# One more gate set in the recurrence of a four-layer kernel, one layer matrix made eleven batches earlier, and one batch's outputs issued in two pairs

## The chip, the core and the metric

The kernel runs on one core of a Trainium2 chip. A core has five engines with instruction streams of their own: TensorE (PE in the profile, with its weight loads shown apart as PEld), VectorE (DVE), ScalarE (ACT), GpSimd (POOL) and SyncE (SP), which here only issues DMA transfers. Each engine takes its instructions in the order in which they were written for it, and they wait for each other through semaphores. All matrices are in 32-bit floats, and the profile shows each such matrix product twice: four products of the program are eight PE instructions in a row.

The metric is the time of one execution on the device in microseconds (us), as the median of several runs.

## The reference

The input x has 16 batches of 512 steps with 512 features each; a condition vector of 512 numbers belongs to each batch. Four layers follow each other, each with a residual: x = x + layer(x, cond).

- L0 scales x by a gate that is worked out from the condition. (Its wavelet transform and the inverse, with one gate for all levels, come to v * gate; the layer has a residual of its own, so x is multiplied by 2 + gate.)
- L1 is a recurrence over the 512 steps: h = tanh(x_t Wx + h Wh + b), with the condition as the first h.
- L2 has three products per batch: f = sigmoid(x Wf + bf), i = sigmoid(x Wi + bi), c = x Wc + bc. With s = f + i, it takes f/s and i/s, multiplies i/s by c, and runs a product over time backwards and a sum over time forwards to get a hidden state per step.
- L3 makes one 512 x 512 matrix per batch, base + A B, where A and B (rank 8) come from a small network on the condition, and multiplies x by it.

## The kernel before

**Phase 1, the recurrence (lines 543 to 677).** The order on PE, ACT, DVE and SP is the order of the program, written out by hand. The 512 steps are 64 blocks (index n) of 8 steps (s). In every step PE issues 16 products h Wh (`accumulate`, L417), ACT takes the tanh (L609) and DVE transposes the result into the next h (L610); then PE may go on with the next step. Between two steps PE is given other work:

- `inputs` (L426 to L432, recorded at L417 too): x Wx for the next block. `SHARE` says how many of its 16 groups go into each step; from block 17 on they are the odd steps 1, 3, 5 and 7, 16 products each.
- `early_gate` (L445 to L522): gate products of L2, for steps of the sequence that are done already. `SETS` lists them: each set is (batches, steps, chunk of 128 features), and has 12 slots, four for f, four for i, four for c. A slot is four products of 32 columns of weights by 512 columns (L465). `PARTS` says in which steps of a block a slot is issued. Before, they are steps 0, 2, 4 and 6 in blocks 17 to 62, and 0, 2, 3, 4 and 6 in block 63.

The elementwise work of a set is cut into pieces for DVE (L488 to L512: two sums, eight inversions of 64 columns, four normalizations, two products with the candidate), and `do_pieces` issues one per step, or two in blocks 62 and 63. The sigmoids on ACT are timed: that of f six steps after its last slot, that of i in the step of its last slot. What is done is written to a DRAM tile `early` with rows of TE steps (L483, on SP's queue). When the last step is over, the pieces that are left are issued, and then `add_base` (L537) for the first batch's L3 matrix.

**Phase 2, batch by batch (lines 680 to 812).** Here a planner orders each engine's instructions. For each of the 16 batches b and each chunk j of 128 features, `gate_unit(b, j, x3)` issues 12 products on PE over the steps that phase 1 did not do (L700; `te` is the number of steps done early), loads the early ones (L715, SP), takes two sigmoids (L716, ACT), and then ten instructions on DVE from L717 to L732, among them a reciprocal (L718) and three scans; two additions on POOL (L736, L737) give `x3`.

Between the units:

- `layer_rows(b)` loads the factors of batch b's L3 matrix (L527, L528, SP) into `at` and `bt`, which have one buffer each.
- `layer_of(b)` (L744) makes the matrix after unit 2: four products into the PSUM banks pl0, pl1, po0 and po1 (L535), and four additions of the base on DVE (`add_base`, L539), which free the banks again.
- `last_layer` (L760) multiplies the previous batch's x3 by its matrix: four tiles of 128 steps, four products each (L756), in turns into the banks po0 and po1; ACT copies each out (L751), SP stores it (L752).

`last_layer` of batch b - 1 stands after unit (b, 1). Batch 15 differs: its own matrix is made after unit (15, 0), in place in `base_sb`, and the outputs of batch 14 stand after unit (15, 3). The outputs of batch 15 follow, three of the four chunks first, the last chunk when DVE has it.

Of the kernel before, what the change touches and what calls it, by code (L numbers as in the profile page):

```python
# [35 lines left out]
P = 128  # L36
B, S, D = 16, 512, 512
KC = D // P
R = 8

T = 8
NBLK = S // T
# [14 lines left out]
FIRST, SECOND, MAIN = 16 // T, 32 // T, 128 // T + 1  # L57
# [3 lines left out]
SETS += [(slice(b, b + 4), slice(0, 128), j) for b in (0, 4) for j in range(KC - 2)]  # L61
SETS += [(slice(b, b + 4), slice(16, 144), KC - 2) for b in (0, 4, 8, 12)]
SETS += [(slice(b, b + 4), slice(32, 160), KC - 1) for b in (0, 4, 8, 12)]
SETS += [(slice(b, b + 4), slice(64, 192), j) for b in (8, 12) for j in (0, 1)]

PARTS = [()] * FIRST + [(0, 1, 3, 4, 5, 7)] * (SECOND - FIRST) + [(0, 2, 4)] * (MAIN - SECOND) + [(0, 2, 4, 6)] * (NBLK - MAIN - 1) + [(0, 2, 3, 4, 6)]
TE = 192


def made_before(b, j):  # L70
# [13 lines left out]
def kernel(  # L84
# [360 lines left out]
    def early_gate(q, step):  # L445
# [32 lines left out]
        def sigmoid(gate, bias):  # L478
            nc.scalar.activation(gate, ps, AF.Sigmoid, bias=col(bias, j))
# [33 lines left out]

        if which == 0:

            timed.setdefault(step if first else step + 6, []).append(lambda: sigmoid(f, C_BF))
        elif which == 1:
            timed.setdefault(step, []).append(end_input_gate)
        else:

            assert not any(job in pieces for job in early_gate.sums)
            urgent.extend(lambda at=at: times_candidate(at) for at in halves)  # L522
# [168 lines left out]
    def bank(tag, name):  # L691
        return pools[tag].tile([P, D], F32, tag=tag, name=f"{tag}_{name}")
# [56 lines left out]
    def leave(b, t, po, tag="osb"):  # L749
        osb = work.tile([P, D], F32, tag=tag, name=f"osb_{b}_{t}")  # L750
        nc.scalar.copy(osb, po)  # L751
        nc.sync.dma_start(out=out[b, t * P : (t + 1) * P, :], in_=osb)  # L752

    def output_part(po, t, x3, layer, ks):
        for k in ks:
            nc.tensor.matmul(  # L756
                po, x3[:, k, t * P : (t + 1) * P], layer[:, k, :], start=(k == 0), stop=(k == KC - 1)
            )

    def last_layer(b, x3, layer):  # L760
        for t in range(S // P):
            po = bank(f"po{t % 2}", f"{b}_{t}")
            output_part(po, t, x3, layer, range(KC))
            leave(b, t, po)

    layer = wx_sb
    pending = None
    for b in range(B):
        x3 = x3pool.tile([P, KC, S], F32, tag="x3", name=f"x3_{b}")
        end = b == B - 1  # L770
        if 0 < b < B - 1:
            factors = layer_rows(b)
        for j in range(KC):
            gate_unit(b, j, x3)
            if j == (KC - 1 if end else 1) and pending is not None:
                last_layer(*pending)
            if j == 2 and 0 < b < B - 1:
                layer_of(b, *factors, layer)
            if j == 0 and end:

                layer_of(B - 1, *layer_rows(B - 1), base_sb)
        pending = b, x3, layer


# [5 lines left out]
    def last_rows(ks, n):  # L790
        for k in ks:
            nc.tensor.matmul(
                ends[n],
                x3[:, k, last * P :],
                base_sb[:, k, columns[n]],
                start=(k == 0),
                stop=(k == KC - 1),
            )

    for t, po in enumerate(pos):  # L800
        output_part(po, t, x3, base_sb, range(KC - 1))
    for n in range(2):
        last_rows(range(KC - 1), n)

    for t, po in enumerate(pos):
        output_part(po, t, x3, base_sb, (KC - 1,))
        leave(B - 1, t, po, ("osb", "i", "s")[t])
    for n, copy in enumerate((nc.vector.tensor_copy, nc.scalar.copy)):
        last_rows((KC - 1,), n)
# [61 lines left out]
```

## Time and profile before

The kernel before took 1618.64 us (median of 3 runs, 1617.01 to 1619.62). The profiled execution took 1615.84 us; its span, from the first to the last instruction, is 1614.1 us.

| what | us |
|---|---|
| phase 1, to the first product of unit (0, 0) at 909.40 | 909.4 |
| phase 2, from there to the end of the span | 704.7 |
| PE busy | 1603.6 (99%) |
| DVE busy | 1132.3 (70%) |
| ACT busy | 424.9 (26%) |
| POOL busy | 172.6 (11%) |

In a line of the profile's timeline stand the start in us from the span's start, the length in us, the engine, the source line, the operation, what it writes <- what it reads (partitions x elements) and how many such instructions are merged (x); brackets at the end name the idle time before and what ended it. L417 is line 417 of the kernel before. The end of a product is modelled, so the distance from one start to the next is what is read from PE's rows, not the length. "PEclk" is the clock that was granted to TensorE, 1.00 being full.

### The profile page before, as it was taken

How to read it: one execution, taken by the hardware profiler on the slowest of the kernel's cores; microseconds unless marked ns; L12 is line 12 of the kernel's file. 1: busy time of each engine (PE TensorE's matmuls, PEld its weight loads, DVE VectorE, ACT ScalarE, POOL GpSimd, SP SyncE). 2: the span in 40 equal slices, each digit the busy share in tenths (PEclk: the TensorE clock that was granted, in tenths of full speed). 3: DMA queues.
4: the chain of work that ended last, by engine and by line, in shares of the span. 5: the costliest groups of instructions: out<-in, count | busy, mean ns of one | idle time of the engine just before them, and what ended most of it. 6: DMA issues, size and time to landing. Idle time of an engine off the chain costs nothing.

```text
span 1614.1 us, 67901 instructions
## 1 busy us (share of the span) xinstructions
PE 1603.6 (99%) x29328; PEld 1146.0 (71%) x29328; DVE 1132.3 (70%) x3618; ACT 424.9 (26%) x2484; POOL 172.6 (11%) x145
## 2 busy tenths in 40 slices
PE   9999999999999999999999999999999999999998
PEld 6888888888888888888888655555555555555564
DVE  4555655565556666666665798888888888988887
ACT  3333333333333333333333211111111111111111
POOL 0000000000000000000000022222222222222222
PEclk9999999999999999999999999999999999999999
DMA  7554431111111111111111101111111111111111
GB/s 228 148 147 128 121 105 46 36 31 36 37 37 37 37 37 37 37 37 31 37 39 30 29 21 43 33 43 39 43 40 44 44 46 39 31 44 47 37 44 58
DMA packets 128085, 88.11 MB, mean 55 GB/s; under 512 B 22645, under 2 KB 116633, under 8 KB 127785
## 3 DMA queue, kind: packets, MB, share of 16 engines
q1 hardware_dynamic: 79152, 55.05, 11.1%
q10 hardware_dynamic: 48632, 28.73, 6.2%
q8 instruction: 229, 3.75, 1.0%
q14 instruction: 72, 0.58, 0.1%
HBM read 55.67 MB, written 28.07 MB: 52 GB/s over the span
## 4 chain that ended last, share of the span: by engine, by line
PE 96%; DVE 2%; DMA 1%; issue 0%; SPq 0%; ACT 0%; ACTq 0%; DVEq 0%
PE pre L417 41%; PE po L756 13%; PE pg L465 13%; PE pf L700 9%; PE pc L700 9%; PE pi L700 9%; PE pf L380 1%; PE pl_layer L535 1%; DVE s L718 1%; DMA wh_sb<-in_wh_dram 1%; PE pl_last L756 0%; DMA xb<-in_xT_dram 0%; DVE s L726 0%; DVE s L730 0%; PE po_last L756 0%
## 5 line engine op out<-in xcount | busy, mean ns | idle before, releaser
L417 PEld LDWEIGHTS pre<-wh_sb,h_out 128*32 128x32 f32 x16384 | 466.7, 110 | 146.6 <-DVE h_out L610 143.4
L417 PE MATMUL pre<-wh_sb,h_out 128*32 128x128 f32 x16384 | 560.6, 273 | 2.4 <-DVE h_out L610 1.1
L610 DVE STREAM_TRANSPOSE h_out<-a 128x32 f32<-128x32 f32 x2048 | 264.6, 187 | 347.4 <-ACT a L609 345.9
L609 ACT ACTIVATE a<-pre 128x32 f32<-128x32 f32 x2048 | 238.0, 203 | 573.4 <-PE pre L417 572.7
L417 PE MATMUL pre<-wx_sb,x 128*32 128x128 f32 x8192 | 285.9, 273 | 1.0 <-DMA wx_sb<-in_wx_dram 0.5
L417 PEld LDWEIGHTS pre<-wx_sb,x 128*32 128x32 f32 x8192 | 239.0, 110 | 2.1 <-DMA wx_sb<-in_wx_dram 1.5
L756 PE MATMUL po<-wx_sb,x 128*128 128x512 f32 x480 | 209.0, 592 | 0.1
L756 PEld LDWEIGHTS po<-wx_sb,x 128*128 128x128 f32 x480 | 91.0, 190 | 111.6 <-issue 105.7
L700 PE MATMUL pf<-x,wf_sb 128*128 128x352 f32 (+3 forms) x512 | 165.3, 466 | 0.3 <-DVE x L622 0.3
L700 PE MATMUL pc<-x,wc_sb 128*128 128x352 f32 (+3 forms) x512 | 163.7, 463 | 1.3 <-DVE i L722 1.3
L700 PE MATMUL pi<-x,wi_sb 128*128 128x352 f32 (+3 forms) x512 | 163.6, 462 | 0.0
L718 DVE RECIPROCAL s<-s 128x368 f32<-128x368 f32 (+2 forms) x64 | 152.2, 2378 | 2.2
L700 PEld LDWEIGHTS pf<-x,wf_sb 128*128 128x128 f32 x512 | 96.0, 190 | 68.4 <-issue 15.8
L736 POOL TENSOR_TENSOR s<-s,f 128x512 f32<-128x512 f32 x63 | 86.5, 1374 | 509.9 <-DVE s L730 504.1
L700 PEld LDWEIGHTS pc<-x,wc_sb 128*128 128x128 f32 x512 | 97.2, 190 | 57.5 <-DVE i L722 1.9
L700 PEld LDWEIGHTS pi<-x,wi_sb 128*128 128x128 f32 x512 | 97.3, 190 | 55.9
L622 DVE TENSOR_TENSOR x<-x,h_out 128x128 f32<-128x128 f32 x256 | 101.2, 395 | 18.9 <-DMA wi_sb<-in_wiT_dram 0.2
L751 ACT COPY osb<-po 128x512 f32<-128x512 f32 x60 | 35.1, 585 | 263.4 <-PE po L756 144.9
L683 POOL MEMSET zero<- 128x1 f32 x1 | 0.1, 98 | 907.5 <-DVE wx_sb L539 907.5
L717 DVE SCALAR_TENSOR_TENSOR s<-f,i 128x368 f32<-128x368 f32 (+2 forms) x64 | 34.7, 543 | 88.1 <-ACT i L716 88.1
L716 ACT ACTIVATE f<-pf,vec_sb 128x368 f32<-128x368 f32 (+2 forms) x64 | 35.7, 558 | 215.2 <-PE pf L700 160.6
L465 PE MATMUL pg<-x,wc_sb 128*32 128x512 f32 (+1 forms) x640 | 84.2, 581 | 0.0
(113 smaller groups left out, 1270.8 us busy)
## 6 DMA issues: line engine op xcount, KB each, us to landing
out_dram<-osb SPq DMA_DIRECT2D x63, 256.0 KB
xb<-in_xT_dram ACTq DMA_DIRECT2D x61, 256.0 KB
w<-in_l3w_dram SPq DMA_DIRECT2D x72, 128.0 KB
w<-in_l3w_dram ACTq DMA_DIRECT2D x64, 128.0 KB
early<-ef SPq DMA_DIRECT2D x39, 128.0 KB
early<-ei SPq DMA_DIRECT2D x39, 128.0 KB
f<-early SPq DMA_DIRECT2D x16, 96.0 KB
i<-early SPq DMA_DIRECT2D x16, 96.0 KB
```

The lines of the kernel that those rows point to most:

```text
L417: nc.tensor.matmul(pre[PLACE[g][0]][j * BP : (j + 1) * BP, PLACE[g][1], :], lhsT, tile_columns(w, j), start=False, stop=False, skip_group_ ...
L465: nc.tensor.matmul(ps[c * BP : (c + 1) * BP, :].rearrange("p (b t) -> p b t", **shape), w[:, k, j * P + c * BP : j * P + (c + 1) * BP], x2 ...
L609: nc.scalar.activation(a[:, at], pre[bank][:, place, at], AF.Tanh)
L610: nc.vector.transpose(turned[:, c, :], a[:, at])
L622: nc.vector.tensor_tensor(x2[:, :, :, at].rearrange("p k b t -> p k t b"), xs[n][:, :, t0 // 2, :, :], turned.rearrange("p k (t b) -> p k ...
L700: nc.tensor.matmul(p[:, te:], w_sb[:, k, j * P : (j + 1) * P], x2[:, k, b, te:], start=(k == 0), stop=(k == KC - 1),)
L716: nc.scalar.activation(gate[:, new], p[:, new], AF.Sigmoid, bias=col(bias, j))
L717: nc.vector.scalar_tensor_tensor(s[:, new], f[:, new], EPS, i[:, new], ALU.add, ALU.add)
L718: nc.vector.reciprocal(s[:, new], s[:, new])
L736: engine.tensor_tensor(s, s, f, ALU.add)
L751: nc.scalar.copy(osb, po)
L756: nc.tensor.matmul(po, x3[:, k, t * P : (t + 1) * P], layer[:, k, :], start=(k == 0), stop=(k == KC - 1))
```

## The change

1. **One more set**, (batches 4 to 7, steps 128 to 255, chunk 0), the seventeenth of now 21. Its 12 slots go into step 7 of blocks 53 to 62, beside the input products that are there, and into steps 1 and 5 of block 63. `made_before(b, 0)` is 256 rather than 128 for these four batches. TE grows from 192 to 256. As the slots of a set now follow each other more closely, the sigmoid of f comes at the latest one step before the first slot of the set's third gate.
2. **The matrix of batch 15** is made in batch 4, after unit (4, 0), and put into `x2[:, :, 0, :]`, the place of batch 0's input to L2; `layer_rows(15)` stands at the head of batch 4. `layer_rows(b)` of the batches 1 to 14 now comes after unit (b, 0).
3. **The outputs of batch 14** stand in two pairs of tiles, after the units (15, 1) and (15, 2). In every batch the products of the first two tiles are interleaved: three of tile 0, two of tile 1, the last of tile 0, the last two of tile 1.

```diff
+SETS += [(slice(4, 8), slice(128, 256), 0)]
 SETS += [(slice(b, b + 4), slice(64, 192), j) for b in (8, 12) for j in (0, 1)]
-PARTS = ... + [(0, 2, 4)] * (MAIN - SECOND) + [(0, 2, 4, 6)] * (NBLK - MAIN - 1) + [(0, 2, 3, 4, 6)]
-TE = 192
+PARTS = ... + [(0, 2, 4)] * (MAIN - SECOND)
+PARTS += [(0, 2, 4, 6)] * (NBLK - MAIN - 11) + [(0, 2, 4, 6, 7)] * 10 + [tuple(range(T - 1))]
+TE = 256
+SLOTS = [n * T + s for n in range(NBLK) for s in PARTS[n]]
+FIRST_PARTS = SLOTS[::KC]
...
-            timed.setdefault(step if first else step + 6, []).append(lambda: sigmoid(f, C_BF))
+            late = step if first else min(step + 6, FIRST_PARTS[u + 2] - 1)
+            timed.setdefault(late, []).append(lambda: sigmoid(f, C_BF))
...
-    def last_layer(b, x3, layer):
-        for t in range(S // P):
-            po = bank(f"po{t % 2}", f"{b}_{t}")
-            output_part(po, t, x3, layer, range(KC))
-            leave(b, t, po)
+    def last_layer(b, x3, layer, rows):
+        t = rows[0]
+        po = [bank(f"po{n}", f"{b}_{t + n}") for n in range(2)]
+        ahead = 0 if t else 2
+        output_part(po[0], t, x3, layer, range(KC - 1))
+        output_part(po[1], t + 1, x3, layer, range(ahead))
+        output_part(po[0], t, x3, layer, (KC - 1,))
+        leave(b, t, po[0])
+        output_part(po[1], t + 1, x3, layer, range(ahead, KC))
+        leave(b, t + 1, po[1])
...
+    last_matrix = x2[:, :, 0, :]
+    when = ({1: ((0, 1), (2, 3))}, {1: ((0, 1),), 2: ((2, 3),)})
...
-        if 0 < b < B - 1:
-            factors = layer_rows(b)
+        extra = layer_rows(B - 1) if b == KC else None
         for j in range(KC):
             gate_unit(b, j, x3)
-            if j == (KC - 1 if end else 1) and pending is not None:
-                last_layer(*pending)
+            if extra and j == 0:
+                layer_of(B - 1, *extra, last_matrix)
+            if j == 0 and 0 < b < B - 1:
+                factors = layer_rows(b)
+            if pending is not None:
+                for rows in when[end].get(j, ()):
+                    last_layer(*pending, rows)
             if j == 2 and 0 < b < B - 1:
                 layer_of(b, *factors, layer)
-            if j == 0 and end:
-                layer_of(B - 1, *layer_rows(B - 1), base_sb)
```

In the last outputs `last_matrix` stands for `base_sb`.

More of the change, by code (lines that the diff above doesn't have):

```diff
@@ L63 @@
 SETS += [(slice(b, b + 4), slice(32, 160), KC - 1) for b in (0, 4, 8, 12)]
+SETS += [(slice(4, 8), slice(128, 256), 0)]
 SETS += [(slice(b, b + 4), slice(64, 192), j) for b in (8, 12) for j in (0, 1)]
-PARTS = [()] * FIRST + [(0, 1, 3, 4, 5, 7)] * (SECOND - FIRST) + [(0, 2, 4)] * (MAIN - SECOND) + [(0, 2, 4, 6)] * (NBLK - MAIN - 1) + [(0, 2, 3, 4, 6)]
-TE = 192
+PARTS = [()] * FIRST + [(0, 1, 3, 4, 5, 7)] * (SECOND - FIRST) + [(0, 2, 4)] * (MAIN - SECOND)
+PARTS += [(0, 2, 4, 6)] * (NBLK - MAIN - 11) + [(0, 2, 4, 6, 7)] * 10 + [tuple(range(T - 1))]
+TE = 256
+SLOTS = [n * T + s for n in range(NBLK) for s in PARTS[n]]
+FIRST_PARTS = SLOTS[::KC]
+assert len(SLOTS) == 3 * KC * len(SETS)
 def made_before(b, j):
@@ L794, in last_rows @@
                 x3[:, k, last * P :],
-                base_sb[:, k, columns[n]],
+                last_matrix[:, k, columns[n]],
                 start=(k == 0),
@@ L800 @@
     for t, po in enumerate(pos):
-        output_part(po, t, x3, base_sb, range(KC - 1))
+        output_part(po, t, x3, last_matrix, range(KC - 1))
     for n in range(2):
@@ L805 @@
     for t, po in enumerate(pos):
-        output_part(po, t, x3, base_sb, (KC - 1,))
+        output_part(po, t, x3, last_matrix, (KC - 1,))
         leave(B - 1, t, po, ("osb", "i", "s")[t])
```

## The prediction

> **What bounds the kernel now.** I read the page's busy shares first, then the chain, then the timeline of PE with that of DVE beside it.
>
> ```profile
> PE 1603.6 (99%) x29328; PEld 1146.0 (71%) x29328; DVE 1132.3 (70%) x3618; ACT 424.9 (26%) x2484; POOL 172.6 (11%) x145
> PE 96%; DVE 2%; DMA 1%; issue 0%; SPq 0%; ACT 0%; ACTq 0%; DVEq 0%
> ```
>
> PE is never without work, and 96% of the chain is PE: what the change adds to PE, or makes PE wait for, goes into the time in full. Next, three steps of the recurrence, and one without a filler near its end:
>
> ```profile
> 863.73 1.09 PE L417 MATMUL pre<-wh_sb,h_out 128*32 128x128 f32 x32
> 864.61 1.07 PE L465 MATMUL pg<-x,wc_sb 128*32 128x512 f32 x8
> 865.47 1.09 PE L417 MATMUL pre<-wh_sb,h_out 128*32 128x128 f32 x32
> 866.34 1.09 PE L417 MATMUL pre<-wx_sb,x 128*32 128x128 f32 x32
> 867.21 1.09 PE L417 MATMUL pre<-wh_sb,h_out 128*32 128x128 f32 x32
> ...
> 896.77 1.09 PE L417 MATMUL pre<-wh_sb,h_out 128*32 128x128 f32 x32
> 898.40 1.08 PE L417 MATMUL pre<-wh_sb,h_out 128*32 128x128 f32 x32 [0.54 <-DVE h_out L610]
> ```
>
> A gate slot takes 0.86 us (864.61 to 865.47), input products 0.87; a step with either is 1.74 us long, a bare one 1.63. So the way over ACT and DVE hides 0.75 us of filler, and one filler already uses it up.
>
> In phase 2 the timelines of PE and DVE belong together (batch 4 starts at 1074.48):
>
> ```profile
> 1074.48 2.74 PE L700 MATMUL pf<-x,wf_sb 128*128 128x384 f32 x8
> 1082.22 2.74 PE L700 MATMUL pf<-x,wf_sb 128*128 128x384 f32 x8
> 1089.96 13.90 PE L756 MATMUL po<-wx_sb,x 128*128 128x512 f32 x32
> 1111.21 0.70 PE L535 MATMUL pl_layer<-bt,at 8*128 8x512 f32 x2
> 1112.28 2.63 PE L700 MATMUL pf<-x,wf_sb 128*128 128x352 f32 x8
> ...
> 1084.49 0.54 DVE L717 SCALAR_TENSOR_TENSOR s<-f,i 128x384 f32<-128x384 f32 x1
> 1093.62 0.54 DVE L717 SCALAR_TENSOR_TENSOR s<-f,i 128x384 f32<-128x384 f32 x1
> 1109.52 0.54 DVE L717 SCALAR_TENSOR_TENSOR s<-f,i 128x368 f32<-128x368 f32 x1 [6.68 <-ACT i L716]
> 1119.37 1.26 DVE L539 TENSOR_TENSOR wx_sb<-po_layer,base_sb 128x512 f32<-128x512 f32 x2
> ```
>
> The reader is to see that DVE lags: PE begins unit (4, 0) at 1074.48, DVE only at 1084.49, a unit costs DVE 9.13 us, and it catches up once per batch (the 6.68 us of idle time). A matrix's additions into po0 and po1 stand behind the whole unit after which it is made: PE's products are at 1111.21, the additions at 1119.37. At the end:
>
> ```profile
> 1574.63 1.26 DVE L539 TENSOR_TENSOR base_sb<-po_layer,base_sb 128x512 f32<-128x512 f32 x2
> 1580.39 2.63 PE L700 MATMUL pc<-x,wc_sb 128*128 128x352 f32 x8 [1.29 <-DVE i L722]
> 1582.86 13.90 PE L756 MATMUL po<-wx_sb,x 128*128 128x512 f32 x32
> ```
>
> Here unit (15, 3) waits 1.29 us for DVE, and PE reuses po0 only at 1582.86.
>
> **The change part by part.** The profiled execution took 1615.84 us, 1.8 more than its span; the median of the runs is 2.8 above it. I work out differences and add them to the median.
>
> *Slots in phase 1.* Step 7 of blocks 53 to 62 has 16 input products, which already cover the 0.75. Ten slots of 0.86 add 8.6. The slots in steps 1 and 5 of block 63 fill bare steps: 2 x (1.74 - 1.63) = 0.2.
>
> *The sigmoids on ACT.* By the new timing those of f and i (0.71 and 0.69 us in their rows) fall into one step three times: step 2 of block 56, 0 of 61, 2 of 63. Tanh is queued behind them, then the transposes, then PE. Tanh begins 1.12 us into a step, the two sigmoids would end about 2.9 after the step's start, and the next tanh is due at 1.74 + 1.12 = 2.86. Bounds: nothing, as now, to three whole sigmoids of 0.6, 1.8. I take 0.2, since the sum nearly closes.
>
> *The end of phase 1.* One piece of DVE is left after the last step now, five in the changed program, with two more inversions in the step itself: some 1.8 us until DVE's last addition (912.57 now). ACT's first f waits for that: 914.5 rather than 912.74. PE wants its bank again at 909.40 + 3 x 2.58 = 917.1, so 2 us of cover remain: nothing. The third gate of the last set now uses the bank that the first matrix's fourth part takes; DVE frees it at 908.33, PE asks at 908.1, and the wait for x at 909.40 covers that.
>
> *Shorter units.* Unit (b, 0) takes PE 1082.22 - 1074.48 = 7.74 with 384 columns; 256 are two thirds, 5.16. Four units: -10.3. (Products of 256 columns stand in the outputs' end at 0.215 us each, half of 512's 0.43.) The loads of these units grow from 64 to 128 KB, and four stores come on SP, all issued when a buffer comes free, units ahead: nothing. The rows of `early` get longer, which touches only these transfers.
>
> *The matrix of batch 15, in batch 4.* Four products, 1.07 us (1111.21 to 1112.28), moved, not added. Its eight loads take the place on SP that batch 4's loads had (from 1067.48 on, 12 us ahead of their use); batch 4's own eight go behind the loads of i for unit (4, 1), issued at 1084.6, and are wanted only after unit (4, 2), past 1100: nothing. But the banks are now wanted soon. PE ends unit (4, 0) at 1079.64, the matrix at 1080.71, unit (4, 1) at 1088.45, and then wants po0 for the outputs of batch 3. DVE takes the additions in its own order: behind unit (3, 3), which ends at 1084.49 as now, the two for pl0 and pl1 lie within unit (4, 0), those for po0 and po1 after its last scan. In the unit of 368 columns the first addition into po0 starts 1119.37 - 1109.52 = 9.85 us after the unit; 112 columns less save 1.17 (0.0105 per column, from 9.13 at 384 to 8.45 at 320), so it starts at 1093.17 and ends 0.67 later at 1093.84. PE waits 5.4 us, and 0.1 to refill. Behind it on PE stand the 16 output products and everything later; ACT's copies wait for them, and DVE for the i of unit (4, 2), where it had 6.7 us of idle time anyway. PE has no idle time later in which to win this back: +5.5.
>
> *The end.* Without the outputs of batch 14 behind it, unit (15, 3) no longer meets a DVE that lags: -1.5 (the products start at 1580.39; 2.37 after the group before at 1576.57 would be 1578.94). What is late next: DVE's last chunk. Its unit ends some 8.7 us after PE's unit (15, 3), and PE has 10.3 us of products to put between; 1.6 us of cover, where now it is 3.4. Nothing. The interleaved products of the first two tiles ask for chunk 3 of x3 two products later, and PE does not wait there now: nothing.
>
> Sum: 8.6 + 0.2 + 0.2 - 10.3 + 5.5 - 1.5 = +2.7.
>
> *The clock after the wait.* No row shows PE idle for 5.4 us within the run; after 1.29 us the eight products went at their usual 2.47. The span's start shows a PE that comes from rest:
>
> ```profile
> L263 PE MATMUL idle<-blank x17: 379/611/634, 1.3 to 10.6; 128*128 128x512 bf16 x17
> ```
>
> The same product took 611 ns there and 379 later. With their mean of 541, 12 of the 17 were slow, and 12 x 0.23 = 2.8 us were lost. So the price lies between 0 and 2.8. I take 1.2: 5.4 us is four times the longest wait shown, but no rest of unknown length. That makes +3.9, 1622.5.
>
> The Trainium skill (TensorE: Matmul & The Clock Gate, HAM oscillation) speaks against this change: PE gaps beyond about 3.4 us throttle TensorE's clock to half until a window of that length was busy. By that rule the wait would cost some 1.7 us more (an estimate from that page), and the sum would be +4.4. The granted clock reads 1.00 even at the span's start, so the granted clock may not show it.
>
> **The rivals.**
>
> - *A, the wait without a slower clock.* +2.7, 1621.3, which is 0.17%: not slower by the bound used here (0.2%, 3.2 us, about what a measurement of this kernel can tell from no change; the three runs spread by 2.6). It decides if the slow stretch costs under 0.5 us. For it: the normal pace after 1.29 us. Against it: the start.
> - *B, no wait in batch 4.* -2.8, 1615.8. For it: pl0 and pl1 are free early. Against it: po0's addition is behind the scans of unit (4, 0) in the changed order, and in batch 15 of the profile it came 15 us after the products (1574.63 against 1559.2).
> - *C, the recurrence pays for the sigmoids.* 1.6 more: +5.5, 1624.1. Against it: ACT is busy a quarter of the time.
> - *D, the slots in step 7 cost nothing.* -8.6 against the forecast: 1613.9. Against it: PE's rows show no gap to put them in.
>
> **How the numbers follow.** Forecast 0.50 (slower 0.47, same 0.03), A 0.25 (same 0.20, slower 0.05), B 0.12 (same 0.09, faster 0.03), C 0.08 slower, D 0.05 faster: slower 0.60, same 0.32, faster 0.08. The forecast's own range runs from A's 1621.3 to both unknown costs at their ends, 2.7 + 2.8 + 1.6 = 7.1, 1625.7. With the runs' scatter of 1.3 on both sides and part of B, I give 1617.5 to 1626.5.
>
> **What would show it.** Step 7 of blocks 53 to 62 at 2.61 us. The four units at 5.16. A PE row of the outputs after unit (4, 1) with about 5.4 us of idle time put down to DVE's addition (L546 in the changed kernel), and products longer or further apart behind it if the clock falls. No wait at unit (15, 3) nor before the last products. The forecast is wrong if that wait is under 3 us, if PE finds new waits at the end, or if steps of block 56, 61 or 63 are longer by a sigmoid.

## The result: 0.6% slower, and the profile after

The kernel after takes 1627.57 us (median of 6 runs, 1626.40 to 1629.88); the kernel before, beside it, 1618.15 us (1617.01 to 1619.62). The ratio is 1.0061, with a 95% interval of 1.0051 to 1.0072: 9.4 us slower. I had said 1622.5 us, slower at 0.60, with a range up to 1626.5. The direction was right; of the size, +3.9 us against 9.4, I had less than half, and the result lies above the range.

The profiled execution of after took 1627.77 us with a span of 1626.0, close to its median; that of before (1615.84, span 1614.1) lay 2.3 below its own. What before's execution had by luck (it kept full clock throughout, as about a third of before's runs did) has to be kept apart from what the change did.

In the kernel after, lines stand 6 or 7 further down than in before: the products h Wh are at L423, the gate slots at L471, the units at L707, the factors' products at L542, the additions at L546, the outputs at L763, the copies at L758 and the stores at L759; POOL's first addition is L743. (In the kernels of the experiments they stand a few lines further up or down.) The page's first lines, busy shares and chain:

```profile
PE 1610.8 (99%) x29423; PEld 1152.4 (71%) x29424; DVE 1134.7 (70%) x3634; ACT 425.0 (26%) x2486; POOL 172.1 (11%) x145
PE 92%; DVE 4%; issue 1%; DMA 1%; ACT 0%; POOL 0%; SPq 0%; ACTq 0%; DVEq 0%
```

PE is still busy for 99%, and that share hides the loss: PE is busy 7.2 us longer, part of it with products that ran slowly. The chain tells more: DVE's part has doubled.

A step 7 with a slot in it, in the timeline of PE:

```profile
874.92 1.06 PE L423 MATMUL pre<-wh_sb,h_out 128*32 128x128 f32 x32
875.80 1.06 PE L423 MATMUL pre<-wx_sb,x 128*32 128x128 f32 x32
876.67 1.04 PE L471 MATMUL pg<-x,wi_sb 128*32 128x512 f32 x8
877.53 1.06 PE L423 MATMUL pre<-wh_sb,h_out 128*32 128x128 f32 x32
```

From 874.92 to 877.53 are 2.61 us, as worked out. Batch 4, on PE and then on DVE:

```profile
1086.76 1.89 PE L707 MATMUL pf<-x,wf_sb 128*128 128x256 f32 x8
1092.03 0.70 PE L542 MATMUL pl_layer<-bt,at 8*128 8x512 f32 x2
1093.10 2.85 PE L707 MATMUL pf<-x,wf_sb 128*128 128x384 f32 x8
1106.34 16.37 PE L763 MATMUL po<-wx_sb,x 128*128 128x512 f32 x32 [5.23 <-DVE x L546]
1122.55 1.71 PE L707 MATMUL pf<-x,wf_sb 128*128 128x368 f32 x5
...
1096.77 0.40 DVE L724 SCALAR_TENSOR_TENSOR s<-f,i 128x256 f32<-128x256 f32 x1
1105.54 1.26 DVE L546 TENSOR_TENSOR x<-po_layer,base_sb 128x512 f32<-128x512 f32 x2
```

This is the predicted wait at the predicted place: the outputs of batch 3 stand for 5.23 us, and DVE's additions into po0 and po1 begin at 1105.54, behind the last scan of unit (4, 0). What follows was priced too low: the 16 output products take from 1106.34 to 1122.55, 16.21 us, where the other batches take 13.73. The clock says why (stretches of the span; PEclk, the granted clock, is the third number from the end):

```profile
1100.00:1104.00 4.00, 1.11 (x4) 0.36 (x2) 4.00 (x7) 0.00 (x0) 0.00 (x0) 1.00 0.08 20
1104.00:1106.00 2.00, 0.00 (x0) 0.00 (x0) 2.00 (x3) 0.00 (x0) 0.31 (x1) 0.59 0.00 0
1106.00:1108.00 2.00, 1.66 (x2) 0.84 (x3) 1.97 (x4) 0.00 (x0) 1.92 (x2) 0.50 0.18 46
1108.00:1110.00 2.00, 2.00 (x4) 0.79 (x3) 1.97 (x2) 0.00 (x0) 0.50 (x1) 0.50 0.16 40
1110.00:1112.00 2.00, 2.00 (x5) 0.94 (x4) 2.00 (x5) 0.00 (x0) 0.00 (x0) 0.71 0.00 0
1112.00:1114.00 2.00, 2.00 (x6) 0.80 (x6) 1.97 (x3) 0.00 (x0) 0.00 (x0) 1.00 0.00 0
```

PE stands from 1101 on, the clock falls to a half at about 1104.4, and for about five of the next 16 us the products run at half pace: 2.48 us lost. The end, on PE:

```profile
1567.25 2.32 PE L707 MATMUL pf<-x,wf_sb 128*128 128x320 f32 x8
1606.06 2.53 PE L707 MATMUL pc<-x,wc_sb 128*128 128x352 f32 x8
1608.42 5.31 PE L763 MATMUL pl_last<-x,x 128*128 128x512 f32 x12
1621.74 0.59 PE L811 MATMUL pi_end<-x,x 128*128 128x256 f32 x2
```

No wait at unit (15, 3) or before the last products. From the first product of unit (15, 0) to the end of the last one are 55.08 us; before they were 57.91, from the first to the last of these rows:

```profile
1552.60 2.32 PE L700 MATMUL pf<-x,wf_sb 128*128 128x320 f32 x8
1609.92 0.59 PE L792 MATMUL pi_end<-base_sb,x 128*128 128x256 f32 x2
```

Of the 2.83 saved, 1.07 are the matrix that moved to batch 4.

What I had not looked for is in batches 8 to 14. These are rows of batch 11 from the timelines of SP, ACT and PE:

```profile
1425.33 0.32 SPq L722 DMA_DIRECT2D f<-early  x1
1425.70 4.16 SPq L759 DMA_DIRECT2D out_dram<-osb  x3
...
1414.07 0.59 ACT L758 COPY osb<-po 128x512 f32<-128x512 f32 x1 [1.13 <-PE po L763]
1428.92 0.59 ACT L758 COPY osb<-po 128x512 f32<-128x512 f32 x1 [8.76 <-DMA out_dram<-osb]
...
1428.21 0.70 PE L542 MATMUL pl_layer<-bt,at 8*128 8x512 f32 x2
1429.56 1.12 PE L542 MATMUL po_layer<-bt,at 8*128 8x512 f32 x2 [0.21 <-ACT osb L758]
1430.61 2.63 PE L707 MATMUL pf<-x,wf_sb 128*128 128x352 f32 x8
```

Tile 1 of the outputs is copied at 1414.07, but its store leaves SP only at 1425.70, because a load of f stands before it in SP's queue; that load waits for the f buffer which POOL's addition frees (1424.04 to 1425.31). Tile 3 needs the osb buffer of tile 1, so ACT's fourth copy waits until 1428.92, and the last of the four matrix products needs the bank that this copy empties. The group of four takes 2.40 us (1428.21 to 1430.61) instead of 1.07. Before, in batch 8, the same copy came three microseconds ahead of the products:

```profile
1285.70 0.58 ACT L751 COPY osb<-po 128x512 f32<-128x512 f32 x1 [7.16 <-DMA out_dram<-osb]
1288.65 0.70 PE L535 MATMUL pl_layer<-bt,at 8*128 8x512 f32 x2
```

The loss is easily missed: the list of PE's waits puts only 0.4 us down to these copies, since most of it shows as longer products.

The two profiles against each other, by starts on PE:

| part | after - before, us | predicted |
|---|---|---|
| opening, up to block 53 of the recurrence | +3.44 | 0 |
| slots, from there to the end of phase 1 | +8.81 | +8.8, and +0.2 for sigmoids |
| four shorter units | -10.24 | -10.3 |
| wait in batch 4 | +5.50 | +5.5 |
| half clock behind it | +2.48 | +1.2 |
| late copies, batches 8 to 14 (4.50 against 1.02) | +3.48 | 0 |
| the end, with the matrix moved | -1.76 | -1.5 |
| sum | +11.71 (the ends of the last products differ by 11.82) | +3.9 |

The wait by starts is counted from 1100.84, where a unit of 7.74 us ends that began at 1093.10, to 1106.34; the row's 5.23 leave out the last product's own time. The opening is 3.4 to 3.8 us later from the 10th block on, before anything of the change but the longer rows comes into play, and 8.3 to 8.4 us are left behind it.

### The profile page after: what moved, and what is told of

It is laid out like the page before. It is cut to its first block, busy times and chain, and to the rows that moved or that the text cites. A ratio compares the mean times of both kernels' runs of the same rounds, so it can differ in the third digit from the quotient of the medians.

```text
span 1626.0 us, 68128 instructions
## 1 busy us (share of the span) xinstructions
PE 1610.8 (99%) x29423; PEld 1152.4 (71%) x29424; DVE 1134.7 (70%) x3634; ACT 425.0 (26%) x2486; POOL 172.1 (11%) x145
## 4 chain that ended last, share of the span: by engine, by line
PE 92%; DVE 4%; issue 1%; DMA 1%; ACT 0%; POOL 0%; SPq 0%; ACTq 0%; DVEq 0%
PE pre L423 41%; PE pg L471 13%; PE po L763 11%; PE pf L707 8%; PE pc L707 8%; PE pi L707 8%; DVE s L725 1%; PE pf L386 1%; DVE s L733 1%; DVE s L737 1%; PE pl_layer L542 1%; DMA xb<-in_xT_dram 1%; PE pl_last L763 0%; DVE i L736 0%; DMA out_dram<-osb 0%
## 5 line engine op out<-in xcount | busy, mean ns | idle before, releaser
L423 PEld LDWEIGHTS pre<-wh_sb,h_out 128*32 128x32 f32 x16384 | 466.0, 110 | 153.7 <-DVE h_out L617 145.9
L423 PE MATMUL pre<-wh_sb,h_out 128*32 128x128 f32 x16384 | 559.9, 273 | 2.1 <-issue 1.2
L423 PE MATMUL pre<-wx_sb,x 128*32 128x128 f32 x8192 | 288.2, 273 | 1.6 <-issue 0.8
L423 PEld LDWEIGHTS pre<-wx_sb,x 128*32 128x32 f32 x8192 | 240.3, 110 | 3.6 <-DMA wx_sb<-in_wx_dram 1.5
L763 PE MATMUL po<-wx_sb,x 128*128 128x512 f32 x480 | 211.1, 598 | 5.2 <-DVE x L546 5.2
L763 PEld LDWEIGHTS po<-wx_sb,x 128*128 128x128 f32 x480 | 92.1, 192 | 117.5 <-issue 112.4
L707 PE MATMUL pf<-x,wf_sb 128*128 128x352 f32 (+4 forms) x512 | 161.9, 459 | 0.0
L707 PE MATMUL pc<-x,wc_sb 128*128 128x352 f32 (+4 forms) x512 | 160.2, 456 | 0.0
L707 PE MATMUL pi<-x,wi_sb 128*128 128x352 f32 (+4 forms) x512 | 160.2, 456 | 0.0
L725 DVE RECIPROCAL s<-s 128x368 f32<-128x368 f32 (+3 forms) x64 | 149.0, 2328 | 2.2
L707 PEld LDWEIGHTS pf<-x,wf_sb 128*128 128x128 f32 x512 | 96.0, 190 | 65.3 <-issue 13.7
L743 POOL TENSOR_TENSOR s<-s,f 128x512 f32<-128x512 f32 x63 | 85.8, 1361 | 509.0 <-DVE s L737 509.0
L707 PEld LDWEIGHTS pc<-x,wc_sb 128*128 128x128 f32 x512 | 97.3, 190 | 52.5
L707 PEld LDWEIGHTS pi<-x,wi_sb 128*128 128x128 f32 x512 | 97.3, 190 | 52.5
L758 ACT COPY osb<-po 128x512 f32<-128x512 f32 x60 | 35.2, 586 | 280.4 <-DMA out_dram<-osb 138.6
L724 DVE SCALAR_TENSOR_TENSOR s<-f,i 128x368 f32<-128x368 f32 (+3 forms) x64 | 34.6, 540 | 91.4 <-ACT i L723 91.4
L471 PE MATMUL pg<-x,wf_sb 128*32 128x512 f32 (+1 forms) x672 | 88.9, 582 | 0.0
L471 PE MATMUL pg<-x,wi_sb 128*32 128x512 f32 (+1 forms) x672 | 88.0, 582 | 0.0
```

The source lines that it names most:

```text
L423: nc.tensor.matmul(pre[PLACE[g][0]][j * BP : (j + 1) * BP, PLACE[g][1], :], lhsT, tile_columns(w, j), start=False, stop=False, skip_group_ ...
L471: nc.tensor.matmul(ps[c * BP : (c + 1) * BP, :].rearrange("p (b t) -> p b t", **shape), w[:, k, j * P + c * BP : j * P + (c + 1) * BP], x2 ...
L707: nc.tensor.matmul(p[:, te:], w_sb[:, k, j * P : (j + 1) * P], x2[:, k, b, te:], start=(k == 0), stop=(k == KC - 1),)
L724: nc.vector.scalar_tensor_tensor(s[:, new], f[:, new], EPS, i[:, new], ALU.add, ALU.add)
L725: nc.vector.reciprocal(s[:, new], s[:, new])
L743: engine.tensor_tensor(s, s, f, ALU.add)
```

## The experiments

My theory after the two profiles: the six terms behind the opening add up, and each can be taken away by itself. The late copies come from a loop. From one fourth copy to the next are DVE's four units with the additions, POOL's addition, the load of f, the store, and the copy, which in turn holds back the sigmoids that DVE needs next. In after that took 42.90 us in each of the batches 8 to 10 (copies at 1299.35, 1342.25 and 1385.15), 0.46 more than PE's 42.44 for a batch. Before, batches 4 to 7 took PE 45.0 and let DVE gain a lead. The rivals: the copies are late because of the new order of loads and pairs, or because of the stall in batch 4; the clock fell for a reason of its own; and the opening is later because of the longer rows.

In the comparisons, before had medians of 1616.44 to 1617.95 us; kernels that were timed together share the same runs of before. "Behind the opening" is the difference of two profiles from the first product of unit (0, 0), or from block 53, on.

**Without the gate set.** Early set, slots, sigmoid timing and row length are before's; matrix and pairs are after's.

```diff
-SETS += [(slice(4, 8), slice(128, 256), 0)]
...
-PARTS += [(0, 2, 4, 6)] * (NBLK - MAIN - 11) + [(0, 2, 4, 6, 7)] * 10 + [tuple(range(T - 1))]
-TE = 256
+PARTS += [(0, 2, 4, 6)] * (NBLK - MAIN - 1) + [(0, 2, 3, 4, 6)]
+TE = 192
...
-            late = step if first else min(step + 6, FIRST_PARTS[u + 2] - 1)
+            late = step if first else step + 6
```

> The kernel after without the gate set: the early set, its ten slots in step 7 and the longer rows of the buffer are as before; the last matrix in batch 4 and the pairs of tiles stay. Theory: unit (4, 0) is 2.6 us longer on PE again, so the wait for the additions in batch 4 falls from 5.2 us to about 3.3 (2.6 less, and some 0.7 more for DVE's wider unit); what the clock loses after it is between 0 and 2.5; the end gives 2.8 back; batches 5 to 7 take 45.0 us, DVE has its slack again, and the waits for copies in batches 8 to 14 are those of before. That is 1618.2 + 3.3 + (0 to 2.5) - 2.8 = 1618.7 to 1621.2. Rival: the waits for copies come from the changed order of loads and from the pairs, not from DVE's lost slack; then they stay, 3.5 us more, 1622.2 to 1624.7, with products into po1 that wait from batch 8 on.

Measured: 1621.96 us, ratio 1.0027 (1.0017 to 1.0038). The number lies by the rival, the profile does not: the copies are on time up to batch 12, and late by 0.5 us in sum after that, less than before's 1.0. So the new order of loads and pairs doesn't make them late. My size was off at the stall, in the timeline of PE:

```profile
1085.27 2.85 PE L701 MATMUL pf<-x,wf_sb 128*128 128x384 f32 x8
1097.18 16.91 PE L757 MATMUL po<-wx_sb,x 128*128 128x512 f32 x32 [3.90 <-DVE x L540]
1113.92 2.64 PE L701 MATMUL pf<-x,wf_sb 128*128 128x368 f32 x8
```

A wait of 4.2 us by starts (3.90 in the row), and 16.74 us for the outputs: 3.0 us lost at half clock after the shorter wait, against 2.5 after the longer one.

**The set alone.** `last_layer` and everything below it as in before.

```diff
-    def last_layer(b, x3, layer, rows):
+    def last_layer(b, x3, layer):
...
-    last_matrix = x2[:, :, 0, :]
...
+            if j == 0 and end:
+                layer_of(B - 1, *layer_rows(B - 1), base_sb)
```

> The gate set alone: the second phase's order, the last matrix's place and the outputs of batch 14 are those of before. Theory: the slots cost 8.8 us, the four shorter units give 10.3 back, and because batches 5 to 7 now take 42.4 us instead of 45.0, DVE falls behind and the copies of batches 8 to 14 come late for some 3.5 us in sum: 1618.2 + 8.8 - 10.3 + 3.5 = 1620.2. Rival: the late copies came from the stall in batch 4 and the four additions there, or from the order of the loads; then they don't show here, and the kernel takes 1616.7 us, faster than before.

Measured: 1618.76 us, ratio 1.0012 (1.0003 to 1.0020), 1.6 us over the median of before and 2.2 behind the opening; the theory said 2.0. The copies are late from batch 7 on (from batch 8 in after), without any stall in batch 4, 4.6 us in sum against before's 1.0. The set by itself spends DVE's lead; it doesn't pay, though it takes 1.4 us of work off PE.

**The matrix in two halves**, two products each into pl0 and pl1, in batches 4 and 5; nobody wants these banks soon.

```diff
+    def half_of(b, at, bt, layer, half):
...
-        extra = layer_rows(B - 1) if b == KC else None
+        extra = layer_rows(B - 1) if b in (KC, KC + 1) else None
...
-                layer_of(B - 1, *extra, last_matrix)
+                half_of(B - 1, *extra, last_matrix, b - KC)   # chunks 2 * half and 2 * half + 1
```

> The kernel after with the last matrix made in two halves, each in the banks pl0 and pl1 alone, after units (4, 0) and (5, 0), from rows that are loaded twice; no output waits for these additions. Theory: the wait of 5.2 us in batch 4 goes, and with it the 2.5 us at half clock, since the clock fell because PE stood still; the late copies of batches 8 to 14 stay (3.5 us against before): 1627.6 - 7.7 = 1619.9. Rival for the clock: it fell for another reason, and stays at half for some 5 us somewhere in batches 4 or 5: 1622.3. Rival for the copies: they were late because of the stall, and go with it: 1616.4.

Measured: 1618.16 us, ratio 1.0008 (0.9999 to 1.0016). Both the wait and the half clock are gone, on PE:

```profile
1091.80 1.13 PE L760 MATMUL pl<-bt,at 8*128 8x512 f32 x4
1098.12 2.74 PE L707 MATMUL pc<-x,wc_sb 128*128 128x384 f32 x8
1100.70 13.90 PE L770 MATMUL po<-wx_sb,x 128*128 128x512 f32 x32
1114.43 2.02 PE L707 MATMUL pf<-x,wf_sb 128*128 128x368 f32 x6
```

13.73 us of outputs at full clock: without the stand, the clock doesn't fall. The late copies stay, though smaller: 3.1 us, from batch 10 on, where I had expected after's 4.5; how much of this difference is the stall and how much the second phase's new order was not separated. What I had put at nothing: a group of two products takes 1.06 us (1091.80 to 1092.86), as long as one of four, so the halves cost 1.25 in each of two batches.

**Own tiles for the outputs.** After batch b, nothing reads x2[:, :, b, :] any more, and it is four tiles wide.

```diff
-        osb = work.tile([P, D], F32, tag=tag, name=f"osb_{b}_{t}")
+        osb = work.tile(...) if b == B - 1 else x2[:, t, b, :]
```

> The kernel after with the outputs of batches 0 to 14 copied into the places of the batch's own four tiles in x2, which nothing reads any more, instead of into two osb tiles: no copy waits for an earlier store. Theory: matrix products into po1 wait in batches 8 to 14 for the fourth copy, and this for the store of tile 1; with own tiles these waits go (4.5 us), the rest stays: 1623.1 us, all seven groups of matrix products take 1.07 us from first to last. Rival: the products wait for the copies because ACT itself is late (its sigmoids wait for DVE); then they stay, and the time is 1627.6.

Measured: 1619.82 us, ratio 1.0021 (1.0010 to 1.0032). Batch 11 on PE:

```profile
1423.31 0.70 PE L542 MATMUL pl_layer<-bt,at 8*128 8x512 f32 x2
1423.32 0.70 PE L542 MATMUL po_layer<-bt,at 8*128 8x512 f32 x2
1424.38 2.04 PE L707 MATMUL pf<-x,wf_sb 128*128 128x352 f32 x6
```

1.07 us, in every batch, and 42.44 from batch to batch: all 4.50 us of late copies are gone. The median fell by more (6.5 by the ratios), since in this profile the same 5.23 us of waiting cost only 1.70 at half clock and the opening was 3.1 earlier.

**Stores from ACT's queue**, with the two osb tiles as they were.

```diff
-        nc.sync.dma_start(out=out[b, t * P : (t + 1) * P, :], in_=osb)
+        (nc.sync if b == B - 1 else nc.scalar).dma_start(out=out[b, t * P : (t + 1) * P, :], in_=osb)
```

> The kernel after with the stores of the outputs of batches 0 to 14 issued from ACT's queue, with the two osb tiles as they are. Theory: in batches 8 to 14 the store of tile 1 stands on SP behind a load of f that waits for POOL; on ACT's queue nothing stands before it, it goes out at once after its copy and has landed before tile 3 is ready: the late copies go as with own tiles, 4.5 us below after, about 6 us above before (1.0037). Rival: the stores themselves take long to land, whoever issues them: then the matrix products still wait, and the time is that of after, 9.4 us above before.

Measured: 1622.91 us, ratio 1.0033 (1.0022 to 1.0044). All matrix groups take 1.07 us here too. So it was SP's order, not the landing of the stores: the store stood behind a load that waited for something else. (5.2 us of waiting cost 2.67 at half clock here.)

**A shorter wait.** Without the set, and with po0 and po1 first in the order of the additions.

```diff
-        for c, pl in enumerate(banks):
+        for c in (2, 3, 0, 1) if layer is not wx_sb else range(KC):
+            pl = banks[c]
```

> The kernel after without the gate set, and with the four additions of the last matrix in the order po0, po1, pl0, pl1: po0 is free two additions (1.26 us) sooner, and the wait in batch 4 falls from 4.2 to 2.9 us. If the clock falls after a wait of this length as well, it costs 1.7 to 3.0 us as before, and the kernel is 1.3 us below the one without the gate set (ratio to before 1.0019). If 2.9 us of standing still are too few for the clock to fall, that loss goes too, and the kernel is 3 to 4.3 us below it (ratio 1.0000 to 1.0009), with PEclk at 1.00 throughout the outputs of batch 3.

Measured: 1617.87 us, ratio 1.0003 (0.9994 to 1.0012). The wait didn't become 2.9 but two of 0.7 and 0.9 by starts, because the planner puts an addition among the instructions of the unit:

```profile
1091.70 2.81 PE L758 MATMUL po<-wx_sb,x 128*128 128x512 f32 x6 [0.42 <-DVE x L541]
1095.10 11.43 PE L758 MATMUL po<-wx_sb,x 128*128 128x512 f32 x26 [0.59 <-DVE x L541]
```

PEclk is 1.00 throughout. The kernel is 4 us below the one without the set; waits of this length cost their length. A wait of 2.9 us wasn't tried after all.

**Both mends**, halves and own tiles, with the set and without it (edits as above).

> The kernel after with both mends: the last matrix in two halves through pl0 and pl1, and the outputs copied into the batch's own tiles. Theory: the terms add. Against before: slots +8.8, four shorter units -10.3, no wait and no half clock in batch 4, no late copies (before has 1.0 us of them, so -1.0), the end -2.8: 5.3 us below before, a ratio of 0.9967. Rival: without these waits DVE is the next bound in the second phase (it has 4.1 us of idle time in a batch of 42.4 us, and gets 1.3 us more in batches 4 and 5), unit starts wait for DVE, and half of that is lost: 2 to 3 us below before.

> As the kernel with both mends, but without the gate set (early set, slots and row length as before). Theory: only the late copies and the end differ from before: -1.0 - 2.8 = 3.8 us below before, a ratio of 0.9977, and the gate set itself is worth 1.5 us where nothing waits behind it (8.8 against 10.3). Rival: the gate set costs more than its units give back even so (sigmoids or stores in the recurrence that I put at nothing): then this kernel is below the one with both mends.

Measured: 1615.01 us, ratio 0.9984 (0.9975 to 0.9992), and 1615.36 us, 0.9989 (0.9980 to 0.9998). Neither DVE nor anything else takes the place of the waits: apart from the halves, all groups and batches are at their bare times. Both fall short of my sum by the 2.5 us of the two halves, which I had left out; with them, in us, the rows of the first give 8.81 - 10.24 + 2.5 - 1.02 - 2.83 = -2.8, and its median is 2.5 below before; those of the second give 2.5 - 1.02 - 2.83 = -1.35, and its median is 2.2 below. The rival on DVE has that number too, but no wait stands in the profile for it. By the rows the set is worth 1.4 us here; the two medians are only 0.35 apart, with intervals of some 1.4 us on either side.

**Own tiles in the kernel before**, by the edit given.

> The kernel before with the outputs of batches 0 to 14 copied into the batch's own tiles. Theory: before has late copies too, only later (from batch 11 on) and 1.0 us in sum; they go, and nothing else changes: 1.0 us below before, a ratio of 0.9994. Rival: own tiles bring more than the waits seen in the profile (ACT and DVE run earlier in every batch): more than 2 us.

Measured: 1616.13 us, ratio 0.9994 (0.9986 to 1.0003): the expected median, though the interval holds no change as well. The profile shows more than expected. Batches 8 to 14 take 42.44 each, and the wait of 1.29 us at unit (15, 3) is gone too, though the outputs of batch 14 still stand behind that unit:

```profile
1580.65 2.53 PE L700 MATMUL pc<-x,wc_sb 128*128 128x352 f32 x8
```

Its opening is 2.74 us later than that of before, and behind the opening it is 2.59 us shorter: 1.02 of late copies, and 1.55 by starts at that unit. So by its profile the rival (more than 2 us) came true; the later opening hides it in the time.

**Longer rows in the kernel before, and after once more.** The first has TE = 256 and nothing else.

> The kernel before with rows of 256 instead of 192 values in the buffer of early gates, and nothing else of the change. If the longer rows are to blame for the later opening of the kernels with the set (3.4 us in the profile of after), the blocks from 13 on are some 2 to 3 us later and the time is 1.0012 to 1.0018 of before. If the opening merely scatters from run to run, the ratio is 1.000 within its interval.

> The kernel after once more, for a second profile beside the same runs of before. Slots 8.8, units -10.3, a wait of 5.2, late copies +3.5 against before and the end -2.8 are the same to a tenth; the loss at half clock is between 1.7 and 3.0; the opening lies anywhere between 0.3 us before and 3.5 us behind that of the kernel before. In the medians 6.1 to 7.4 us above before and what the openings differ by in the mean (0 to 2).

Measured: 1617.31 us, ratio 1.0006 (0.9995 to 1.0016), which leaves room for up to 2.6 us; and 1625.36 us, ratio 1.0053 (1.0040 to 1.0065), with 2.31 us in the opening, 1.70 at half clock in batch 4 and 7.1 us behind the opening. Its late copies had something new, in stretches of the span:

```profile
1426.00:1428.00 2.00, 1.70 (x8) 0.60 (x8) 0.00 (x0) 1.16 (x3) 0.00 (x0) 1.00 0.48 183
1428.00:1430.00 2.00, 2.00 (x6) 1.01 (x5) 1.50 (x2) 0.36 (x1) 0.00 (x0) 0.83 0.38 141
1430.00:1432.00 2.00, 2.00 (x4) 1.07 (x4) 2.00 (x3) 0.00 (x0) 0.00 (x0) 0.50 0.07 21
1432.00:1434.00 2.00, 2.00 (x7) 1.26 (x6) 2.00 (x6) 0.55 (x1) 0.00 (x0) 0.81 0.00 0
```

The group of batch 11 took 2.48 us, and behind it the clock was at half for 3.4 us, which cost another 1.70. In the first profile of after, a group of 2.40 in the same batch was followed by full clock.

**The whole matrix at the head of batch 1.** Batch 0 makes no matrix in phase 2, so the four banks are free there. The outputs go into own tiles, by the edit above.

```diff
-        extra = layer_rows(B - 1) if b == KC else None
+        extra = layer_rows(B - 1) if b == 1 else None
+        if b == 1:
+            layer_of(B - 1, *extra, last_matrix)
...
-            if extra and j == 0:
-                layer_of(B - 1, *extra, last_matrix)
```

> The kernel after with own tiles, and with the whole last matrix made at the head of batch 1, ahead of unit (1, 0), where the four banks are free (batch 0 makes no matrix in phase 2) and DVE takes the additions before unit (1, 0). Theory: its four products cost 1.07 us as in after, against 2.5 for the two halves (each group of two took as long as a group of four); DVE stands some 3.5 us for the last chunk of batch 0, and has 4.7 us of idle time in batch 1 to take it from, so PE waits nowhere: 1.4 us below the kernel with both mends, 4 us below before (0.9975). Rival: DVE comes so late that PE waits in batch 1 or 2 for a sigmoid or an addition, 1 to 3 us, and the kernel is at or above the one with both mends.

Measured: 1613.43 us, ratio 0.9979 (0.9969 to 0.9989), no wait in phase 2. Here batch 0's own tiles are also the place of the last matrix, so batch 15 was multiplied by a wrong matrix; the next kernel sends batch 0 through the osb tiles (`if b in (0, B - 1)`), once with the set and once without it.

> The kernel before this, mended: the outputs of batch 0 go through the two osb tiles, those of batches 1 to 14 into their own tiles (in the run before, the copies of batch 0's outputs overwrote the last matrix, so batch 15 was multiplied by a wrong one; the instructions were the same). Theory: the time of that run, 1613.4 us beside 1616.9 of before, ratio 0.9979; PE stands nowhere in the second phase. Rival: a wait for the last additions that the overwritten matrix hid: 1 to 2 us more.

> The same without the gate set. Theory: behind the opening the set is worth 1.4 us (slots 8.8, units 10.25), so this kernel is 1.4 us slower than the one with the set. Rival: the set costs about 1 us in the opening through its longer rows, which the second phase's profile does not show: then the two are within 0.5 us of each other, and the openings (the difference to before at the 53rd block of the recurrence) are later with the set by that much.

Measured: 1615.62 us, 0.9988 (0.9979 to 0.9997), and 1617.19 us, 0.9999 (0.9990 to 1.0007). The set is worth 1.6 us by these medians and 1.36 behind the opening by the profiles, as its rows say (8.81 against 10.24). Whether its longer rows cost something in the opening stays open: these medians speak against it, those of the kernels with both mends leave room for 1 us, and the openings of the eleven profiles with the longer rows are 1.8 us behind before's in the mean, of the five others with short rows 1.1, each group scattering by 3 us. The rival of the first came true at another place: batch 1's matrix group meets a late copy of batch 0's last tile, 1.3 us longer, and in both profiles 3.4 us at half clock follow, 3.0 us in all. With the set, on PE:

```profile
989.24 1.12 PE L542 MATMUL po_layer<-bt,at 8*128 8x512 f32 x2 [0.22 <-ACT osb L758]
990.29 4.33 PE L707 MATMUL pf<-x,wf_sb 128*128 128x352 f32 x8
```

and in stretches of the span:

```profile
988.00:990.00 2.00, 1.78 (x8) 0.48 (x8) 0.00 (x0) 1.40 (x3) 0.00 (x0) 1.00 0.36 136
990.00:992.00 2.00, 2.00 (x4) 1.09 (x4) 1.74 (x2) 0.11 (x1) 0.00 (x0) 0.60 0.39 142
992.00:994.00 2.00, 2.00 (x5) 1.15 (x4) 2.00 (x3) 0.00 (x0) 0.00 (x0) 0.55 0.06 20
```

**Batch 0's stores from ACT's queue**, so that its copies aren't late.

```diff
-        nc.sync.dma_start(out=out[b, t * P : (t + 1) * P, :], in_=osb)
+        (nc.sync if b else nc.scalar).dma_start(out=out[b, t * P : (t + 1) * P, :], in_=osb)
```

> The kernel with the whole matrix at the head of batch 1 and batch 0's outputs through two osb tiles, with batch 0's four stores issued from ACT's queue. Theory: the fourth copy comes early, batch 1's matrix products take 1.08 us without a wait, the clock stays at 1.00 behind them, and the time is that of the run whose copies overwrote the matrix: ratio 0.9979, some 3.5 us below before. Rival: the half clock in batch 1 comes from the eight-row products themselves or from DVE's four additions there, and stays: 0.9988.

Measured: 1612.24 us, ratio 0.9967 (0.9955 to 0.9979): 5.3 us below before by the ratio, 3.98 behind the opening. The page's chain:

```profile
PE 99%; DMA 1%; SPq 0%; issue 0%; ACT 0%; DVE 0%
```

The clock stays at 1.00 in batch 1, and nothing stands in the second phase. The set, the pairs and an early matrix are in this kernel, though the matrix stands in batch 1 and not in batch 4, and it beats both: what the change set off cost more than its parts gave. How much each part gives has to be read beside own tiles in the kernel before, which were 2.59 below before behind the opening. The 3.98 are 1.4 more, and that is the set (1.36). Beyond own tiles, the early matrix and the pairs bring nothing that these profiles show, since own tiles alone take away the wait at unit (15, 3).

## Why the prediction came out too low

*Right, to a tenth or two:* the slots in step 7 (8.8 worked out, 8.81 measured, and the same 8.8 in every kernel with the set); the shorter units (10.3, 10.24); the wait in batch 4, its place, releaser and length (5.5, 5.50 by starts); the end (1.5, 1.76, though own tiles alone take away the same wait); the sigmoids at nearly nothing (0.2 taken; the slots' whole difference leaves nothing for them). Rival B, no wait, and rival D, slots at no cost, fell in the first profile; rival C, the recurrence paying for the sigmoids, with them. Rival A, the wait at full clock, fell in the four profiles with a wait of 5.2 us and the one of 3.9.

*Mis-sized: "The clock after the wait … I take 1.2".* It cost 2.48, 1.70, 1.70 and 2.67 us after the wait of 5.2, and 3.0 after that of 4.2. My bounds of 0 to 2.8 were right for the former, my choice between them was not: I took the middle where the only row of a rested PE, the opening, spoke for the upper end. The Trainium skill (TensorE: Matmul & The Clock Gate, HAM oscillation) says that a gap beyond about 3.4 us throttles. An estimate from it had been 1.7; these waits agree with it, with 3.4 us at half clock or twice that. My remark that the granted clock may not show it was wrong: it reads 0.50. The 1.00 at the span's start was no reading: in before's trace the record of the clock begins only at 6.65 us, where the products of the start pass from 634 ns to 379.

*Wrong: "The loads of these units grow …, all issued when a buffer comes free, units ahead: nothing".* I priced loads and stores on SP by when their data are wanted, not by what stands before them in the queue. The store of tile 1 stands behind a load that waits for DVE and POOL. And I counted DVE's 6.7 us of idle time per batch as cover without asking what a batch shorter by 2.56 us leaves of it. The set alone makes it 3.6 us more of late copies; own tiles or another queue for the stores takes all 4.5 away. The upper end of the range had room for the clock (2.8) and the sigmoids (1.6), and none for copies; without their 3.48 us the result would lie inside it. (With the scatter of 1.3 that I named, that end would be 1627.0 and not 1626.5, and the result is above that too.)

*The opening and the medians.* I added differences to the median of three runs, and no term stood for the opening. In the sixteen profiles beside that of before it came 0.27 us earlier to 3.44 later. Most of this goes with a half clock as well: in eight profiles PEclk is at half somewhere from 14 to 22 us, once for twice as long, and there the opening is 2.4 us late in the mean (0.2 to 3.4), against 0.7 in the eight others (-0.3 to 1.8). These are rows of after, in stretches; before stands at 1.00 in all of them:

```profile
14.00:16.00 2.00, 1.34 (x24) 0.54 (x24) 0.00 (x0) 0.17 (x1) 0.00 (x0) 0.87 1.10 353
16.00:18.00 2.00, 1.92 (x40) 1.63 (x40) 0.49 (x4) 0.47 (x4) 0.00 (x0) 0.50 1.13 322
18.00:20.00 2.00, 2.00 (x64) 1.93 (x60) 0.58 (x2) 0.18 (x3) 0.00 (x0) 0.77 0.77 241
```

It comes with the set and without it (without: in three of six profiles; with: in five of ten). What sets it off there wasn't tried. The mean granted clock is on record for every run, not only the profiled ones: of before's 123 runs in these comparisons, the 39 at 1.000 took 1615.9 us in the mean, the 51 at 0.999 1617.5 and the 30 at 0.998 1618.7. A thousandth is 3.2 us at half clock, so much of the scatter of the medians is half clock; after's six runs read 0.996 to 0.998.

So of the 9.4 us, 8.3 to 8.4 are the terms of the first profile behind its opening; the second profile has 7.1 for a median of 8.9. The 1 to 2 us between lie within the scatter of openings and half clocks, and were not traced further.

## What to carry to other kernels

Before a stage is made shorter, list which other engines' loops run through it, queue order included: the slack of the engine that lags is spent first, and the next wait shows up batches later. A transfer in a queue is as late as whatever stands before it (one store here by 11 us), so put stores that free buffers where no load waits for another engine. And a wait on PE is priced with the clock behind it: here waits of 4 us and more cost 1.7 to 3.0 us on top.

## What was unexpected on the chip

- *Half clock in portions.* PEclk read 1.00 or 0.50, with values between only in stretches that hold a change. Where nothing stood, the loss was 1.70 us, 3.4 us at half; behind the waits of 4 to 5 us it was one or two such portions, part of which fell into the wait itself. The same wait of 5.2 us in the same kernel cost 2.48 in one execution and 1.70 in another. The traces suggest why: in all 17 of them, the changes of clock lie whole multiples of 3.413 us apart, so one can cut each trace into portions of that length (1085.44 us, or 318 portions, lie between two half stretches in after). In the execution with 2.48 the clock fell 2.0 us before the wait ended, PE worked for only 1.42 us of that portion, and a second one at half clock followed; in the one with 1.70 it fell 0.14 us before the end, and one portion was all.
- *Short stalls can do it too.* Matrix groups of eight-row products that took 2.4 us instead of 1.07 were followed by half clock in three profiles (batch 1 twice, batch 11 once) and by full clock in others (batch 11 in the first profile of after). No half clock followed the waits of 0.7 and 0.9 us in the kernel with the shorter wait, nor that of 1.29 in before's unit (15, 3). The Trainium skill's 3.4 us, in the section named above, is no safe bound here. Where a stall lay among the portions of 3.413 us separates these cases. Behind the opening, the clock fell after eight portions, in which PE worked for at most 1.03 us on products other than the eight-row ones (0 to 0.42 at the five long waits, 0.93, 1.00 and 1.03 at the three groups). It fell after none in which PE did so for 1.17 us or more; the portion with 1.17 holds a group of 2.73 us, in batch 12 of the kernel with the set alone. No run was made to test this.
- *Two eight-row products take as long as four.* Two into pl0 and pl1 took 1.06 us, four into four banks 1.07.
